# Neighbour lists ahead of the layers: the product of adjacency and column numbers on GpSimd, one block ahead of VectorE's Max8

## The chip, the cores and the metric

The kernel runs on one NeuronCore of a Trainium2 chip. The metric is the device time of one execution in microseconds (us); the time of a kernel is the median of its runs. TensorE multiplies matrices and transposes, VectorE and ScalarE do elementwise work and reductions, GpSimd does elementwise work too and issues the gathers, SyncE issues loads. Each engine works through its own queue in the order in which the program was written, and stops at an instruction whose semaphores are not there yet.

## The reference: a graph network of four layers

The inputs are `x`, 3327 nodes of 256 features, and `adj`, a 3327 x 3327 matrix of zeros and ones with a one in about 1 of 208 places. Layer 0 is a graph attention with one score per row, layers 1 to 3 are transformers whose attention is masked by `adj`:

```python
# layer 0
h = x @ Wt.T + bt
s = leaky_relu(h @ Wa.T + ba, 0.2)
w = softmax(where(adj > 0, s, NEG), axis=1)
x = layernorm(x + (w @ h) @ Wp.T + bp) * gamma + beta
# layers 1, 2, 3 (8 heads of 32)
q, k, v = split(layer_norm(x, g1, be1) @ w_qkv)
scores = where(adj != 0, einsum('nhd,mhd->hnm', q, k) * SCALE, -inf)
x = x + (softmax(scores) @ v) @ w_proj + b_proj
x = x + gelu(layer_norm(x, g2, be2) @ w1 + b1) @ w2 + b2
```

## The kernel before

A row of `adj` has about 16 ones and, in the data at hand, at most 40. The kernel therefore makes, for each row, the list of its columns, and the attention of layers 1 to 3 gathers only the keys and values on that list. The program has two stages: the one ahead of the layers, which makes the lists and computes layer 0, and the three layers. (A general path for denser matrices is not taken with this data.)

Ahead of the layers the rows are worked in 26 blocks of 128, and four blocks make a group. One block goes through these steps (class `Block`):

- `load`: SyncE loads 128 rows of `adj`, as integers (`a32`, three buffers).
- `sign`: a memset sets the one column that pads 3327 to 3328 (L711; on VectorE for the first three blocks, on GpSimd for the rest), then ScalarE writes the signs as bf16 into `abf` (L714; three buffers).
- `turn`: TensorE transposes `abf` in 26 pieces and ScalarE copies them out (L723, L724). `sums` then multiplies the transposed pieces with the rows of layer 0.
- `candidates`: VectorE multiplies `abf`, seen as 16 segments of 208 columns, with the row of column numbers 1 to 208, `seg1` (L731; the product goes to `v`, of which there are two buffers). 16 Max8 instructions then take the eight largest of each segment into `cand` (L735), that is, the numbers of the columns that hold a one.
- `list`: VectorE adds to each candidate the offset of its segment (L741, L742, both with two inputs) and draws from the 128 candidates the 40 largest, eight at a time, with Max8 and a match-and-replace between them (L746, L748).

A group goes through a dozen steps of its own (class `Group`): `soft` and `mix` are the softmax weights of layer 0 (from L889 and L938 on; L892 makes the one-hot row of the number of neighbours), `add`, `norm` and `norm1` the layer norms, `turn1`, `qkv` and `store` what layer 1 needs. A plan written out by hand (`plan`) gives each of them a place: before the Max8 of some block, or before its list.

Blocks 0 to 3 are done in a lead-in, together with the projection `h` of layer 0. A loop over blocks 4 to 25 does the rest. In turn i of the loop the program issues, in this order: load and sign of block i+2, the group steps of place 2i, the candidates of block i, transposes of block i+2 and (every other turn) the sums, the group steps of place 2i+1, the list of block i. The order on each engine is the order of the program; only buffers are given out by the framework, which puts a wait in front of the first instruction that uses a buffer again. `v` also serves, under the same tag and so out of the same two buffers, some large tiles of the lead-in (`s_h_rest`, `s_h_wa`).

In the layers GpSimd issues 1344 gathers of keys and values (L1303), VectorE forms scores and weighted values (L1325, L1326, L1366), TensorE sums the values over the neighbours and does the projections. A tile's query sits in PSUM, and so do the weights of blocks with short lists (`w`); for blocks with long lists the weights are in SBUF (`sc`).

Of the kernel before, what the change touches and what calls it, by code (L numbers as in the profile page):

```python
# [9 lines left out]
BF = mybir.dt.bfloat16  # L10
# [7 lines left out]
P = 128  # L18
# [14 lines left out]
NB = (N + P - 1) // P  # L33
# [16 lines left out]
NSEG = 16  # L50
SEG = NB * P // NSEG
# [457 lines left out]
@with_exitstack  # L509
def kernel(ctx: ExitStack, tc: tile.TileContext, ins, out: bass.AP):  # L510
    nc = tc.nc
    keep = ctx.enter_context(tc.tile_pool(name="s_keep", bufs=1))
    dram = ctx.enter_context(tc.tile_pool(name="s_dram", bufs=1, space=DRAM))
    flag = keep.tile([1, 1], I32, name="flag")
    E = mybir.EngineType
    with tc.manual_schedule(engines={E.PE, E.DVE, E.Activation, E.Pool, E.SP}):
        with ExitStack() as inner:
            sparse_path(inner, tc, ins, out, dram, flag)
    unfit = nc.values_load(flag[0:1, 0:1])
    with tc.If(unfit > 0):  # L520
        general_path(tc, ins, out)


def sparse_path(ctx, tc, ins, out, dram, flag):
    nc = tc.nc
# [40 lines left out]
    class Norm:  # L566
# [18 lines left out]
        def turn(self, j, v, work, pb):  # L585

            xn = work.tile([P, D], FP, tag="xn", name=f"xn_{self.name}_{j}")
            nc.scalar.activation(xn, v, AF.Identity, bias=self.nm[:, j:j + 1],  # L588
                                 scale=self.rs[:, j:j + 1])
            for c in range(2):  # L590
                nc.tensor.transpose(pb[c][:, j * P:(j + 1) * P], xn[:, c * P:(c + 1) * P], ident)  # L591
# [31 lines left out]
    with tc.tile_pool(name="a", bufs=1) as a, tc.tile_pool(name="aw", bufs=2) as aw, \  # L623
# [10 lines left out]
        seg1 = a.tile([P, SEG], BF, name="seg1")  # L634
# [17 lines left out]
        part = a.tile([P, 1], FP, name="part")  # L652
# [41 lines left out]
        class Block:  # L694
# [21 lines left out]
            def turn(self, aT):  # L716

                i = self.i
                for k0 in range(0, NB, 7):
# [3 lines left out]
                        nc.tensor.transpose(pt[:, m, :], self.abf[:, k * P:(k + 1) * P], ident_bf)  # L723
                    nc.scalar.copy(aT[:, k0:k0 + len(ks), :], pt[:, :len(ks), :])  # L724

            def candidates(self, part=None):

                i = self.i
                if not part:
                    v = self.v = aw.tile([P, NSEG, SEG], BF, tag="v", name=f"s_v_{i}")  # L730
                    nc.vector.tensor_mul(v, self.abf.rearrange("p (s c) -> p s c", c=SEG),  # L731
                                         seg1[:, None, :].to_broadcast([P, NSEG, SEG]))
                    self.cand = aw.tile([P, NSEG, 8], FP, tag="cand", name=f"cand_{i}")
                for s in range(NSEG) if part is None else range(part * 4, part * 4 + 4):
                    nc.vector.max(out=self.cand[:, s, :], in_=self.v[:, s, :])  # L735
# [46 lines left out]
        def x_turn(g):  # L782
            blocks = GROUPS[g]
            xT = aw.tile([P, 2, 512], FP, tag="hT", name=f"s_xT_{g}")
            for c in range(2):
                pb = bank(f"s_px_{g}_{c}")
                for j, i in enumerate(blocks):
                    nc.tensor.transpose(pb[:, j * P:(j + 1) * P],
                                        x_sb[:, i, c * P:(c + 1) * P], ident)
                nc.scalar.copy(xT[:, c, :len(blocks) * P], pb[:, :len(blocks) * P])  # L790
            turned[g] = xT

        def h_of(g):
            blocks, xT = GROUPS[g], turned.pop(g)
            ph = bank(f"s_ph_{g}").rearrange("p (b h) -> p b h", h=H0)
            for j, i in enumerate(blocks):
                for c in range(2):
                    nc.tensor.matmul(ph[:, j, :], xT[:, c, j * P:(j + 1) * P],
                                     S.wtT[:, c, :], start=(c == 0), stop=(c == 1))
            full = [j for j, i in enumerate(blocks) if ROWS[i] == P]  # L800
            for j0, j1, r in ((0, len(full), P), (len(full), len(blocks), ROWS[-1])):
                if j1 > j0:
                    i0 = blocks[j0]
                    nc.vector.tensor_add(
                        S.h[:r, i0:i0 + j1 - j0, :], ph[:r, j0:j1, :],
                        S.bt_b[:r, None, :].to_broadcast([r, j1 - j0, H0]))
# [34 lines left out]
        class Group:  # L841
# [8 lines left out]
            def sums(self, half, aT):  # L850

                c0 = half * 2 * P
                for k in range(NB):
                    r = ROWS[k]
                    nc.tensor.matmul(self.pa[:, c0:c0 + 2 * P], S.hs[:r, k, :P], aT[:r, k, :],  # L855
                                     start=(k == 0), stop=(k == NB - 1))
                    nc.tensor.matmul(self.pc[:H0 + 1, c0:c0 + 2 * P], S.hs[:r, k, P:], aT[:r, k, :],
                                     start=(k == 0), stop=(k == NB - 1))
# [170 lines left out]
        blk = [Block(i) for i in range(NB)]  # L1029
# [28 lines left out]
        for g in range(NG):  # L1058
            x_turn(g)
            if g:  # L1060
                h_of(g - 1)
            if g == 2:
                turn(3)
            if g == 4:
                blk[4].load()
                blk[4].sign()
            for _ in range(2 if g > 3 else 1):
                pieces.pop(0)()
        h_of(NG - 1)
# [34 lines left out]
        def step(g, name):  # L1104
            G = groups[g]
            G.qkv(int(name[3:])) if name[:3] == "qkv" else getattr(G, name)()

        for i in range(4, NB):
            if i + 2 < NB:
                blk[i + 2].load()  # L1110
                blk[i + 2].sign()
            for s in plan[2 * i]:
                step(*s)
            blk[i].candidates()
            if i + 2 < NB:
                turn(i + 2)
                if i % 2 or i + 2 == NB - 1:
                    sums(i + 2)
            for s in plan[2 * i + 1]:
                step(*s)  # L1120
            blk[i].list()
# [512 lines left out]
```

## Time and profile before

| what | value |
|---|---|
| time, median of 3 runs | 2568.74 us (2565.74 to 2574.27) |
| profiled execution | 3158 us, span 3156.3 us |
| busy, share of the span: PE, DVE, ACT, POOL | 57%, 61%, 25%, 43% |
| L731, product on VectorE | 26 instructions, 49.0 us, 1883 ns each |
| L735, Max8 on segments | 416 instructions, 118.0 us, 360 ns each |
| L746, Max8 in the list | 130 instructions, 38.3 us, 295 ns each |
| L714, signs on ScalarE | 26 instructions, 77.4 us, 2978 ns each |
| L711, memset of the padding on GpSimd | 23 instructions, 2.2 us, 104 ns each |

The profile is of one execution, which took longer than the timed ones; it serves for shares, durations and order. PE is TensorE's matmul, PEld its weight load, DVE VectorE, ACT ScalarE, POOL GpSimd. The stage ahead of the layers takes about the first 500 us of the span, and the loop over blocks 4 to 25 of it runs from 86 us to about 455 us. A digit in the busy rows is the busy share of one of 40 equal slices, in tenths.

### The profile page before, as it was taken

How to read it: one execution, taken by the hardware profiler on the slowest of the kernel's cores; microseconds unless marked ns; L12 is line 12 of the kernel's file. 1: busy time of each engine (PE TensorE's matmuls, PEld its weight loads, DVE VectorE, ACT ScalarE, POOL GpSimd, SP SyncE). 2: the span in 40 equal slices, each digit the busy share in tenths (PEclk: the TensorE clock that was granted, in tenths of full speed). 3: DMA queues.
4: the chain of work that ended last, by engine and by line, in shares of the span. 5: the costliest groups of instructions: out<-in, count | busy, mean ns of one | idle time of the engine just before them, and what ended most of it. 6: DMA issues, size and time to landing. Idle time of an engine off the chain costs nothing.

```text
span 3156.3 us, 24036 instructions
## 1 busy us (share of the span) xinstructions
PE 1794.0 (57%) x7561; PEld 1163.5 (37%) x7561; DVE 1935.3 (61%) x3983; ACT 774.6 (25%) x1316; POOL 1362.7 (43%) x1458
## 2 busy tenths in 40 slices
PE   4767752255666666671457667666713435665556
PEld 3645531133333333350334333433512323433334
DVE  6688995457657656533656756755446556656554
ACT  4455621012222222230112212222300111212112
POOL 4000004545555554305555555544054555565550
PEclk9868766577787886785578778878755766776768
DMA  5334306645555565415455555555064554554560
GB/s 207 131 117 148 129 31 204 174 138 169 165 172 162 156 174 152 112 51 177 141 156 156 163 160 150 175 152 140 24 189 125 156 155 135 169 163 147 161 156 13
DMA packets 144486, 453.80 MB, mean 144 GB/s; under 512 B 29521, under 2 KB 40156, under 8 KB 141021
## 3 DMA queue, kind: packets, MB, share of 16 engines
q0 software_dynamic: 113056, 370.26, 40.9%
q1 hardware_dynamic: 9834, 53.90, 4.9%
q10 hardware_dynamic: 21458, 28.02, 2.5%
q8 instruction: 61, 1.00, 0.1%
q14 instruction: 77, 0.63, 0.1%
HBM read 420.64 MB, written 31.42 MB: 143 GB/s over the span
## 4 chain that ended last, share of the span: by engine, by line
DVE 25%; issue 18%; PE 18%; another core or an unknown queue 17%; POOL 11%; ACT 5%; DMA 5%; DVEq 0%; ACTq 0%; POOLq 0%; SPq 0%
POOL kv L1303 11%; DVE kv L1325 5%; DMA kv<-kv,t 4%; DVE sc L1326 3%; DVE vw L1366 3%; PE pu L1439 3%; PE po L1372 3%; PE py L1462 2%; DVE cand L735 2%; PE pk L1492 1%; PE s_pk L1010 1%; ACT s_aT L724 1%; DVE s_v L731 1%; PE pf L591 1%
## 5 line engine op out<-in xcount | busy, mean ns | idle before, releaser
L1303 POOL DMA_INDIRECT kv<-kv,t x1344 | 1273.0, 947 | 1210.3 <-issue 534.2
L1372 PE MATMUL po<-s_ident,vw 128*128 128x128 f32 x2688 | 475.4, 334 | 580.2 <-DVE vw L1366 387.2
L1372 PEld LDWEIGHTS po<-s_ident,vw 128*128 128x128 f32 x2688 | 395.5, 174 | 724.1 <-issue 373.5
L1325 DVE TENSOR_TENSOR kv<-kv,q 128x1024 f32<-128x1024 f32 (+3 forms) x363 | 413.1, 1138 | 397.1 <-ACT q L1311 274.6
L1366 DVE TENSOR_TENSOR vw<-kv,w 128x1024 f32<-128x1024 f32 x333 | 371.4, 1128 | 87.2 <-remote 84.6
L1326 DVE TENSOR_REDUCE sc<-kv 128x32 f32<-128x1024 f32 (+3 forms) x363 | 414.1, 1141 | 12.4
L1439 PE MATMUL pu<-fT,s_w 128*128 128x512 f32 (+3 forms) x768 | 341.2, 579 | 62.3 <-issue 35.8
L1462 PE MATMUL py<-gT,s_w 128*128 128x512 f32 (+2 forms) x672 | 321.8, 597 | 58.1 <-issue 50.2
L1400 DVE TENSOR_TENSOR t<-t,po 128x256 f32<-128x256 f32 x78 | 32.6, 418 | 390.8 <-remote 254.5
L1445 ACT ACTIVATE gT<-pu,pvb 128x512 f32<-128x512 f32 (+3 forms) x192 | 115.7, 607 | 628.2 <-remote 384.1
L1439 PEld LDWEIGHTS pu<-fT,s_w 128*128 128x128 f32 x768 | 157.4, 222 | 196.1 <-issue 146.4
L1462 PEld LDWEIGHTS py<-gT,s_w 128*128 128x128 f32 x672 | 132.6, 206 | 180.7 <-issue 144.0
L1396 PEld LDWEIGHTS po<-s_w_proj,oT 128*128 128x128 f32 x312 | 71.8, 255 | 281.8 <-issue 272.3
L1394 PE MATMUL po<-bias,s_ones_bf 96*128 96x256 bf16 x78 | 25.2, 324 | 259.7 <-issue 147.4
L1390 ACT COPY oT<-po 128x256 f32<-128x256 f32 x78 | 28.9, 371 | 548.5 <-remote 320.2
L711 POOL MEMSET s_abf<- 128x1 bf16 x23 | 2.2, 104 | 361.4 <-DVE s_v L731 253.7
L1492 PE MATMUL pk<-s_w_qkv,nT 128*128 128x512 f32 x208 | 128.4, 748 | 22.0 <-ACT nT L596 9.9
L735 DVE MAX8 cand<-s_v 128x8 f32<-128x208 bf16 x416 | 118.0, 360 | 0.9
L1396 PE MATMUL po<-s_w_proj,oT 128*128 128x256 f32 x312 | 113.1, 500 | 0.0
L723 PE MATMUL s_ptb<-s_ident_bf,s_abf 128*128 128x128 bf16 x676 | 67.1, 265 | 68.3 <-ACT s_abf L714 45.2
L591 PE MATMUL pf<-s_ident,xn_f 128*128 128x128 f32 x156 | 46.1, 444 | 86.8 <-ACT xn_f L588 66.7
L855 PE MATMUL s_pa<-s_aT,s_hs 128*128 128x256 bf16 x338 | 82.3, 290 | 13.2 <-DVE s_hs L817 13.2
(288 smaller groups left out, 2252.1 us busy)
## 6 DMA issues: line engine op xcount, KB each, us to landing
s_a<-in_adj_dram SPq DMA_DIRECT2D x25, 1663.5 KB
kv<-kv,t POOLq DMA_INDIRECT x1344
kv<-kvr ACTq DMA_DIRECT2D x52, 256.0 KB
kv<-s_kvr ACTq DMA_DIRECT2D x26, 256.0 KB
s_w<-in_L_gnn_w_dram SPq DMA_DIRECT2D x6, 1024.0 KB
t<-ql ACTq DMA_DIRECT2D x6, 592.0 KB
t<-s_x ACTq DMA_DIRECT2D x6, 512.0 KB
s_w_qkv<-in_L_gnn_w_qkv_dram SPq DMA_DIRECT2D x3, 768.0 KB
```

Source lines behind the costliest of these rows:

```text
L735: nc.vector.max(out=self.cand[:, s, :], in_=self.v[:, s, :])
L855: nc.tensor.matmul(self.pa[:, c0:c0 + 2 * P], S.hs[:r, k, :P], aT[:r, k, :], start=(k == 0), stop=(k == NB - 1))
L1303: nc.gpsimd.indirect_dma_start(out=t[:, s, :], out_offset=None, in_=kv[L], in_offset=bass.IndirectOffsetOnAxis(ap=t2[:, b, k:k + 1].bitcas ...
L1325: nc.vector.tensor_mul(k, k, self.q[b][:, None, :].to_broadcast([P, n, D]))
L1326: nc.vector.tensor_reduce(self.sc[b][:, s0:s0 + n, :], k.rearrange("p s (h d) -> p s h d", d=HD), AX.X, ALU.add)
L1366: nc.vector.tensor_mul(vw[:, :n * D].rearrange("p (s h d) -> p s h d", h=HEADS, d=HD), v, self.wp[b][:, s0:s0 + n, :, None].to_broadcast([ ...
L1372: nc.tensor.matmul(self.po[b][:, k * P:(k + 1) * P], vw[:, at:at + P], ident, is_transpose=True, start=(s0 + s == 0 and k == 0), stop=(s0 ...
L1396: nc.tensor.matmul(ps, c["oT"][:, k * P:(k + 1) * P], w["w_proj"][:, k, :], start=False, stop=(k == 1))
L1439: nc.tensor.matmul(c["pu", f][:, :n], w["w1"][:, e, f * P:(f + 1) * P], c["hT"][:, e, :n], start=(e == 0), stop=(e == 1))
L1445: nc.scalar.activation(g[:, :n], c.pop(("pu", f))[:, :n], AF.Gelu_apprx_tanh, bias=w["b1"][:, f:f + 1])
L1462: nc.tensor.matmul(c["py"][e][:, :n], w["w2"][:, f, e * P:(e + 1) * P], g[:, :n], start=(f == 0), stop=last)
L1492: nc.tensor.matmul(ps[:, :c1 - c0], c["hT"][:, e, j * P:(j + 1) * P], nxt["w_qkv"][:, e, c0:c1], start=(e == 0), stop=(e == 1))
```

## The change

The product of L731 becomes a function of its own, `weigh`, which takes the engine. For blocks 0 to 3 VectorE makes the product as before. For blocks 4 to 25 GpSimd makes it, and the call stands one turn of the loop earlier: in turn i, ahead of the group steps and of the Max8 of block i, GpSimd is given the product of block i+1. Block 4's is issued in the lead-in, as soon as its sign has been. The purpose is to take the product off VectorE, which has most of the work here, and to have it ready when the Max8 need it. Nothing else is changed: the Max8, the lists and all buffers with their number stay. After the change GpSimd's queue in the loop is, turn by turn, the memset of L711 for block i+2 and the product of block i+1; VectorE's queue is as before without the 22 products. A product waits for the sign of its block (ScalarE) and for a free `v`, that is, for the last Max8 of the block two before it; the first Max8 of a block waits for GpSimd.

```diff
+            def weigh(self, engine):
+
+                v = self.v = aw.tile([P, NSEG, SEG], BF, tag="v", name=f"s_v_{self.i}")
+                engine.tensor_mul(v, self.abf.rearrange("p (s c) -> p s c", c=SEG),
+                                  seg1[:, None, :].to_broadcast([P, NSEG, SEG]))
+
             def candidates(self, part=None):
 
                 i = self.i
+                if i < 4 and not part:
+                    self.weigh(nc.vector)
                 if not part:
-                    v = self.v = aw.tile([P, NSEG, SEG], BF, tag="v", name=f"s_v_{i}")
-                    nc.vector.tensor_mul(v, self.abf.rearrange("p (s c) -> p s c", c=SEG),
-                                         seg1[:, None, :].to_broadcast([P, NSEG, SEG]))
                     self.cand = aw.tile([P, NSEG, 8], FP, tag="cand", name=f"cand_{i}")
...
             if g == 4:
                 blk[4].load()
                 blk[4].sign()
+                blk[4].weigh(nc.gpsimd)
...
             if i + 2 < NB:
                 blk[i + 2].load()
                 blk[i + 2].sign()
+            if i + 1 < NB:
+                blk[i + 1].weigh(nc.gpsimd)
             for s in plan[2 * i]:
                 step(*s)
             blk[i].candidates()
```

## The prediction

> **What bounds the kernel now.** I read the busy rows over the span first, to find where the change lies, then the windows of that stage, VectorE's waits in it, and last the instructions in order of time.
>
> The page's second part has one digit for each 78.9 us:
>
> ```profile
> PE   4767752255666666671457667666713435665556
> DVE  6688995457657656533656756755446556656554
> POOL 4000004545555554305555555544054555565550
> ```
>
> The change lies in slices 1 to 6, ahead of the layers: VectorE (DVE) is the fullest engine there and GpSimd (POOL) is empty until the gathers start. The windows answer cuts the stage finer; its columns are the window, its length, busy us of PE, PEld, DVE, ACT and POOL with the number of instructions, the TensorE clock, the DMA share and GB/s:
>
> ```profile
> 86.00:118.00 32.00, 26.97 (x240) 24.82 (x239) 16.67 (x52) 13.36 (x13) 0.20 (x2) 0.88 0.37 123
> 118.00:200.00 82.00, 50.62 (x368) 39.71 (x367) 67.57 (x257) 42.37 (x51) 0.41 (x4) 0.69 0.34 122
> 200.00:300.00 100.00, 75.44 (x493) 56.61 (x491) 81.89 (x288) 60.35 (x78) 0.61 (x6) 0.80 0.43 150
> 300.00:400.00 100.00, 71.17 (x518) 55.59 (x515) 93.49 (x341) 60.24 (x73) 0.61 (x6) 0.80 0.37 124
> 400.00:455.00 55.00, 28.98 (x168) 19.89 (x169) 51.82 (x203) 17.64 (x31) 2.97 (x2) 0.69 0.11 40
> ```
>
> VectorE is busy 295 of the 337 us between 118 and 455, and what it really waits for there is little (engine and line, waited for, us, times, longest):
>
> ```profile
> DVE s_z L938 <- ACT s_m L919: 7.6, 2, 4.4
> DVE s_x L972 <- PE s_pp L963: 6.8, 3, 5.0
> DVE deg L889 <- ACT s_acc L876: 6.1, 1, 6.1
> DVE place L927 <- PE places L903: 5.6, 2, 2.9
> DVE s_x L986 <- ACT s_x L980: 1.5, 1, 1.5
> ```
>
> 27.6 us in all; the remaining 14 us or so are gaps of 0.03 to 0.2 us between dependent small instructions. So an instruction more or less on VectorE moves the end of the stage, and the layers start after it. One block in order of time (start, us, engine, line, operation):
>
> ```profile
> 308.67 1.88 DVE L731 TENSOR_TENSOR s_v<-s_abf,seg 128x3328 bf16<-128x3328 bf16 x1
> 310.59 4.53 DVE L735 MAX8 cand<-s_v 128x8 f32<-128x208 bf16 x16
> 315.15 0.29 DVE L741 SCALAR_TENSOR_TENSOR ctmp<-cand,off 128x128 f32<-128x128 f32 x1
> 315.48 0.29 DVE L742 TENSOR_TENSOR ctmp<-cand,ctmp 128x128 f32<-128x128 f32 x1
> 315.81 0.29 DVE L746 MAX8 lists<-ctmp 128x8 f32<-128x128 f32 x1
> ```
>
> The product takes 1.88 us, the 16 Max8 4.53 us, the list after them 3.8 us, then the group's steps. What matters below: L741 and L742, right after the last Max8, each read two tiles from SBUF.
>
> [...] beside GpSimd's gathers a product with both inputs in SBUF is no slower than one with its weights in PSUM (`w`):
>
> ```profile
> L1366 DVE TENSOR_TENSOR vw<-kv,w 128x1024 f32<-128x1024 f32 x279 | 336.4, 1215 | 87.2 <-remote 84.6 <-PE pk L1492 0.9
> L1366 DVE TENSOR_TENSOR vw<-kv,sc 128x1024 f32<-128x1024 f32 x30 | 35.0, 1221 | 10.9 <-PE po L1372 10.9
> ```
>
> [...] ahead of the layers GpSimd does only memsets. [...]
>
> **The change part by part.** Removed from VectorE: 22 products, blocks 4 to 25. The Max8 follow at 1.92 us after the product's start, so 22 x 1.92 = 42 us. Block 4's share buys nothing: after it VectorE waits for ScalarE's sign of block 5 until 108.0. Blocks 6 to 25 give 20 x 1.92 = 38 us.
>
> Added on GpSimd: 22 products of 128x3328 bf16, two inputs in SBUF. The trace has no such row. [...] for the upper end I take a quarter more, 9.0 us, should bf16 or the repeated row `seg1` cost something. GpSimd's one-input select of 128x128 in the trace, 0.29 us for 128, would be 7.5 us for 3328, on the same scale. I take 7.3.
>
> Queue and waits: GpSimd's queue is now memset of block i+2, product of block i+1. The product waits for the sign of i+1 and for one of two `v` buffers, that is for the last Max8 of block i-1. It is needed at the first Max8 of block i+1, after list i-1, Max8 i and list i: 3.8 + 4.5 + 3.8 = 12 us at least, so 7.3 us are in time and 9.0 too. Behind the product stands the next memset, and behind that ScalarE's sign two blocks ahead; the memset waited for VectorE's product before, so this is about even: nothing. One product is on the path whatever happens: block 5's sign ends at 107.96, so its Max8 start at 108.0 + 7.3 + 0.15 = 115.4 and not at 109.99, 5.4 us later. Without contention: 5.4 - 38 = -33 us.
>
> [...] the last Max8 of block i-1 releases the GpSimd product. GpSimd's memset started 0.15 us after the product it waited for (310.55 to 310.70). L741 starts at 0.03 us and lasts 0.29, [...] and L742, due 0.04 us later, stands until the product is through. That is 7.3 - 0.1 = 7.2 us, once in nearly every block of 7 to 25. Where the group's softmax steps come between (five blocks), its first two-input instruction, L892, is due 0.4 us on: the same. For block 6, and in part 7, the product is set by a late sign and falls on Max8 and waits. I laid GpSimd products of 7.3 us over VectorE's 380 us of instructions by these rules: 135 us of standing, or 18.7 x 7.2. Sum: -33 + 135 = +102. While VectorE stands, TensorE and ScalarE go on, and of its 27.6 us of waits those that do not hang on its own last instruction, half, go: -14. Result +88 us, 2568.7 + 88 = 2657. [...] with 9.0 it is +140 - 14 = +126 (2695).
>
> The layers are unchanged, in order and in instructions. The profiled execution is longer (3156 us) than the timed ones, and the profile doesn't show where; VectorE's rows in this stage are plain arithmetic, and I take their us as those of the timed runs.
>
> **The rivals.**
> Faster, no contention: two-input instructions of VectorE and GpSimd run side by side. For it speaks that the product has 12 us of room and GpSimd is idle. The gain is at most 33 us. In parts of the stage the chain goes through TensorE and ScalarE (the chain of waits between 90 and 460 gives the product 6.4%, 23.7 us, not 42), so at least 24 - 5 = 19. Middle: -27, 2542. [...]
> Late lock: [...] so L742 slips by. Then 3.1 us of one-input list and, where no steps follow, 4.5 us of Max8 hide the product, and only blocks with steps stand. The same laying-over gives +24, less 14: +10, 2579. The memset's 0.15 us speaks against it; a product may need longer to start than a memset.
> GpSimd as the bound: it would take a product above 12 us. Nothing prices it so high; it would be 2700 and more.
>
> **How the numbers follow.** Contention from L742 on 0.52, late lock 0.12, no contention 0.33, GpSimd the bound 0.03. The time is the first's, 2657. The range must reach into the no-contention case, whose chance is above 0.2: 2534 to 2705 leaves out the best part of that case (0.1) and the top of the first (0.06). Slower by over 0.3% (7.7 us): the first and the last case, 0.55, and half of the late lock, 0.61; the late lock's other half is split between within 0.3% and faster, 0.03 each; of the no-contention case 0.03 ends within 0.3% and 0.30 faster. So within 0.3%: 0.06; faster: 0.33.
>
> **What would show it.** Right: 22 GpSimd TENSOR_TENSOR near 7 us; 22 fewer L731 on VectorE; gaps of some 7 us ahead of L742 (or L742 itself long), ending as a GpSimd product ends, with Max8 at its old 0.36 us; the stage's end, 455 before, at 540 or so. Wrong: L742 at 0.29 us beside a running GpSimd product (no contention), or standing only in group steps (late lock). A product far from 7.3 us scales the result by 19 us for each us.

## The result, and the profile after: 56 us longer, nearly all of it ahead of the layers

| what | before | after |
|---|---|---|
| time, median | 2569.88 us (2565.74 to 2574.27, 4 runs) | 2626.36 us (2624.96 to 2630.80, 4 runs) |
| ratio | | 1.0222, 95% interval 1.0201 to 1.0244 |
| last Max8 on segments ends, in the profile | 453.0 us | 505.7 us |
| first gather of the layers | 504.5 us | 556.9 us |

The change makes the kernel slower by 56.5 us; the interval of the ratio puts it between 52 and 63 us. The stage ahead of the layers is 52.7 us longer at its last Max8 and 52.4 us longer at the first gather. The few us that remain can't be placed: the profiled execution of the kernel before is longer in its layers than any timed one, so the layers of the two traces can't be compared. From the first gather to the end, the profiled execution after takes 2070 us (2627.1 less 556.9), and a timed one of before about 2065 (2569.9 less the 504.5 of the stage), which is an estimate.

The busy rows of the page after, a digit for each 65.6 us:

```profile
PE   5558665523676887787156887778633655775676
DVE  6699999957879888873588888888537877777863
POOL 5233333137777777750677676767127767776770
```

GpSimd is no longer empty ahead of the layers (digits 3 in slices 3 to 7), and VectorE is full there. The windows answer of the kernel after, with the columns as for the kernel before:

```profile
118.00:200.00 82.00, 44.71 (x344) 36.30 (x342) 71.85 (x241) 38.23 (x45) 30.82 (x10) 0.67 0.28 102
200.00:300.00 100.00, 70.78 (x451) 54.46 (x449) 95.78 (x261) 55.02 (x73) 32.65 (x10) 0.76 0.42 147
300.00:400.00 100.00, 63.66 (x394) 47.82 (x395) 96.20 (x242) 45.83 (x56) 39.13 (x12) 0.74 0.32 113
400.00:500.00 100.00, 62.00 (x362) 45.11 (x362) 95.02 (x302) 40.03 (x56) 28.89 (x7) 0.69 0.18 56
```

From 200 us on VectorE is busy 95 or 96 of every 100 us, though it has 22 instructions fewer, and its waits for others have nearly gone (engine and line, waited for, us, times, longest):

```profile
DVE s_z L943 <- ACT s_m L924: 3.3, 1, 3.3
DVE deg L894 <- ACT s_acc L881: 1.6, 1, 1.6
DVE place L932 <- PE places L908: 1.1, 1, 1.1
DVE s_x L977 <- issue: 0.2, 1, 0.2
```

These are 6.2 us where there were 27.6. So the time is in VectorE's own instructions, and the instructions in order of time show in which. First one block on VectorE, then GpSimd in the same stretch:

```profile
331.95 4.52 DVE L740 MAX8 cand<-s_v 128x8 f32<-128x208 bf16 x16
336.50 0.29 DVE L746 SCALAR_TENSOR_TENSOR ctmp<-cand,off 128x128 f32<-128x128 f32 x1
336.83 6.46 DVE L747 TENSOR_TENSOR ctmp<-cand,ctmp 128x128 f32<-128x128 f32 x1
343.32 0.29 DVE L751 MAX8 lists<-ctmp 128x8 f32<-128x128 f32 x1
```

```profile
336.64 6.50 POOL L729 TENSOR_TENSOR s_v<-s_abf,seg 128x3328 bf16<-128x3328 bf16 x1 [13.30 <-DVE cand L740]
```

L747 is the line that was L742: the second instruction of the list, with two tiles from SBUF. It took 0.29 us and takes 6.46 us here. The last Max8 ends at 336.47, GpSimd's product starts 0.17 us later, in the middle of L746, and ends at 343.14; 0.15 us after that L747 is done. L746 ahead of it and the Max8 behind it have their old 0.29 us. Where the group's softmax steps come between, the first instruction with two inputs after the product's start is L897 (L892 before), and it is the one that is held. L896 started 0.06 us before that product, at 393.39, and L912 comes after its end, so these two say nothing of instructions with one input:

```profile
393.33 0.17 DVE L896 TENSOR_SCALAR s_top<-deg 128x4 f32<-128x4 f32 x1
393.53 6.51 DVE L897 TENSOR_TENSOR OH<-num,s_top 128x164 bf16<-128x164 f32 x1
399.96 0.16 DVE L912 TENSOR_SCALAR s_non<-deg 128x4 f32<-128x4 f32 x1
```

The groups of the loop give the whole count, first those of the kernel before (118 to 453 us), then those of the kernel after (118 to 506 us):

```profile
L742 DVE TENSOR_TENSOR ctmp<-cand,ctmp 128x128 f32<-128x128 f32 x20 | 5.8, 292 | 0.7
L892 DVE TENSOR_TENSOR OH<-num,s_top 128x164 bf16<-128x164 f32 (+1 forms) x7 | 2.2, 318 | 0.2
```

```profile
L729 POOL TENSOR_TENSOR s_v<-s_abf,seg 128x3328 bf16<-128x3328 bf16 x20 | 129.7, 6483 | 227.3 <-DVE cand L740 160.4 <-DVE deg L894 31.0 <-ACT s_aT L724 13.3
L747 DVE TENSOR_TENSOR ctmp<-cand,ctmp 128x128 f32<-128x128 f32 x20 | 79.8, 3988 | 0.7
L897 DVE TENSOR_TENSOR OH<-num,s_top 128x164 bf16<-128x164 f32 (+1 forms) x7 | 33.1, 4730 | 0.2
```

L747 takes 79.8 us where L742 took 5.8 in the same 20 blocks, and L897 33.1 where L892 took 2.2: 74.0 and 30.9, together 104.9 us of standing. They are 12 instructions of L747 and 5 of L897, about 6.17 us each: GpSimd's 6.48 us less the 0.3 us that the instruction takes anyway.

Two shorter cases add 3.0 us. One is an instruction with two inputs, L943, held for 1.9 us. The other is a copy of 128x4 with one input, which takes 1.25 us where its usual time is 0.15; it ends as the product beside it does (116.23 to 122.72):

```profile
121.53 1.25 DVE L894 COPY deg<-s_acc 128x4 f32<-128x4 f32 x1 [1.56 <-ACT s_acc L881]
```

### The profile page after: what moved, and what is told of

The parts are those of the page before. It is cut to its first block, busy times and chain, and to the rows that moved or that the text cites. A ratio compares the mean times of both kernels' runs of the same rounds, so it can differ in the third digit from the quotient of the medians.

```text
span 2625.2 us, 24056 instructions
## 1 busy us (share of the span) xinstructions
PE 1694.4 (65%) x7561; PEld 1135.1 (43%) x7561; DVE 2009.3 (77%) x3961; ACT 781.2 (30%) x1316; POOL 1503.6 (57%) x1480
## 4 chain that ended last, share of the span: by engine, by line
DVE 14%; DMA 13%; PE 10%; POOL 9%; issue 8%; ACT 2%; DVEq 0%; POOLq 0%; ACTq 0%
DMA kv<-kv,t 12%; POOL kv L1311 9%; DVE kv L1333 4%; DVE vw L1374 3%; DVE sc L1334 3%; PE pu L1447 3%; PE py L1470 2%; PE po L1380 2%; PE pk L1500 1%; POOL out_dram L1513 0%; PE pq L1500 0%; DMA out_dram<-t,perm 0%; DVE t L1488 0%; PE py L1463 0%; PE po L1404 0%
## 5 line engine op out<-in xcount | busy, mean ns | idle before, releaser
L1380 PE MATMUL po<-s_ident,vw 128*128 128x128 f32 x2688 | 453.1, 327 | 497.4 <-DVE vw L1374 495.9
L1380 PEld LDWEIGHTS po<-s_ident,vw 128*128 128x128 f32 x2688 | 379.7, 169 | 626.3 <-DVE vw L1374 487.8
L1447 PE MATMUL pu<-fT,s_w 128*128 128x512 f32 (+3 forms) x768 | 321.5, 554 | 5.9 <-ACT gT L1453 3.3
L729 POOL TENSOR_TENSOR s_v<-s_abf,seg 128x3328 bf16<-128x3328 bf16 x22 | 142.6, 6482 | 287.8 <-DVE cand L740 160.4
L1470 PE MATMUL py<-gT,s_w 128*128 128x512 f32 (+2 forms) x672 | 286.6, 555 | 0.0
L1500 PE MATMUL pk<-s_w_qkv,nT 128*128 128x512 f32 x208 | 118.7, 700 | 7.2 <-ACT nT L596 7.2
L588 ACT ACTIVATE xn_f<-t,nm_f,rqy_f 128x256 f32<-128x256 f32 x78 | 43.0, 593 | 202.4 <-DVE nm_f L582 196.1
L723 PEld LDWEIGHTS <-s_abf 128*128 128x128 bf16 x676 | 60.2, 128 | 88.5 <-ACT s_abf L714 69.2
L1348 ACT ACTIVATE sc<-sc,mx 128x120 f32<-128x120 f32 (+6 forms) x78 | 32.0, 410 | 221.8 <-DVE mx L1345 219.0
L1404 PE MATMUL po<-s_w_proj,oT 128*128 128x256 f32 x312 | 96.9, 440 | 0.0
```

The lines of the kernel that those rows point to most:

```text
L729: engine.tensor_mul(v, self.abf.rearrange("p (s c) -> p s c", c=SEG), seg1[:, None, :].to_broadcast([P, NSEG, SEG]))
L1380: nc.tensor.matmul(self.po[b][:, k * P:(k + 1) * P], vw[:, at:at + P], ident, is_transpose=True, start=(s0 + s == 0 and k == 0), stop=(s0 ...
L1447: nc.tensor.matmul(c["pu", f][:, :n], w["w1"][:, e, f * P:(f + 1) * P], c["hT"][:, e, :n], start=(e == 0), stop=(e == 1))
L1470: nc.tensor.matmul(c["py"][e][:, :n], w["w2"][:, f, e * P:(e + 1) * P], g[:, :n], start=(f == 0), stop=last)
L1500: nc.tensor.matmul(ps[:, :c1 - c0], c["hT"][:, e, j * P:(j + 1) * P], nxt["w_qkv"][:, e, c0:c1], start=(e == 0), stop=(e == 1))
```

## The experiments: what holds VectorE, and where a GpSimd product costs nothing

The theory, from the trace after: a VectorE instruction with two inputs in SBUF stands until a GpSimd instruction that reads SBUF is through (L747, 6.46 us instead of 0.29); the changed kernel releases its GpSimd product just where two such instructions come next. The rivals: the loss is queueing (late signs, Max8 that wait for a slow engine); GpSimd slows VectorE whatever either of them does; only two-input instructions of both engines clash. All line numbers are those of each kernel, which shift by a few; names of tiles tell what is what. "Standing" is the time that instructions of the loop take above their usual duration. The edits are shown against the changed kernel, but those of the memset and the copy against the kernel with the product on both engines, and those of the last kernel and of the one without a product against the kernel before. The kernels were timed in groups with a kernel before in each (median 2569.9 us for the changed kernel, 2570.2 for the four below it, 2566.6 for the last three), so each ratio is to its own.

| kernel | time, us | ratio to before, 95% interval | last Max8 ends, us | standing, us |
|---|---|---|---|---|
| before | 2566.6 to 2570.2 | | 453.0 | 0 |
| after | 2626.4 | 1.0222 (1.0201 to 1.0244) | 505.7 | 108 |
| product on both engines | 2670.4 | 1.0395 (1.0365 to 1.0426) | 551.4 | 115 |
| GpSimd memset instead | 2579.4 | 1.0032 (1.0012 to 1.0052) | 459.6 | 13 |
| GpSimd copy instead | 2604.8 | 1.0140 (1.0110 to 1.0169) | 488.2 | 45 |
| no product | (other gathers) | | 432.3 | 0 |
| candidates in PSUM | 2614.5 | 1.0182 (1.0153 to 1.0210) | 498.2 | 42 |
| product released after L742 | 2574.7 | 1.0025 (1.0017 to 1.0033) | 457.1 | 27 |
| product in two pieces | 2554.5 | 0.9949 (0.9928 to 0.9969) | 435.0 | 2 |

**The product on both engines.** GpSimd's work is put in without anything being taken out, so queueing and standing come apart.

```diff
-                if i < 4 and not part:
-                    self.weigh(nc.vector)
+                if not part:
+                    self.weigh(nc.vector) if i < 4 else self.product(nc.vector)
```

`product` is the multiplication of `weigh` alone, into the buffer that GpSimd has filled already.

> GpSimd makes the products of blocks 4 to 25 where the changed kernel has them, and VectorE makes them again, as before the change, into the same buffer; so nothing is taken off VectorE. Theory (VectorE's two-input instructions stand while a GpSimd product reads SBUF): the 17 standings of the changed kernel come back whole, L742 and L892 at about 6.5 us, 105 us in all, less about 20 us of waits that go: last Max8 at about 545 us instead of 453, time about 2660. Rival (the loss comes from late signs or from Max8 waiting for GpSimd): VectorE never waits for GpSimd's result here except at block 5, so 2570 to 2580.

The groups of its loop:

```profile
L732 POOL TENSOR_TENSOR s_v<-s_abf,seg 128x3328 bf16<-128x3328 bf16 x20 | 130.6, 6531 | 87.8 <-DVE cand L743 46.6 <-DVE deg L897 27.9 <-ACT s_aT L724 9.0
L750 DVE TENSOR_TENSOR ctmp<-cand,ctmp 128x128 f32<-128x128 f32 x20 | 85.9, 4295 | 0.7
L732 DVE TENSOR_TENSOR s_v<-s_abf,seg 128x3328 bf16<-128x3328 bf16 x21 | 39.5, 1881 | 17.2 <-POOL s_abf L711 17.2
L900 DVE TENSOR_TENSOR OH<-num,s_top 128x164 bf16<-128x164 f32 (+1 forms) x7 | 33.1, 4731 | 0.2
```

L750 is L742. 13 of its 20 instructions and 5 of L900 stand, about 6.2 us each, as in the changed kernel, and VectorE waits 17.2 us for GpSimd's queue (L711), once, at block 5, where it waited 11.3 us for the sign before. The time is 100 us above the kernel before, 10 more than expected, as 115 us stood and not 105. Queueing as the cause is out; it would have been 10 us. The run shows the other order of the two engines as well: a GpSimd product that starts at 118.32, while VectorE's own product is running (117.54 to 119.43), takes 7.45 us instead of 6.48. There it is GpSimd that stands.

**A GpSimd memset in its place.** Writes only.

```diff
-                self.product(engine)
+                if engine is nc.gpsimd:
+                    nc.gpsimd.memset(v, 0.0)
+                else:
+                    self.product(engine)
```

> As the run before, with a GpSimd memset of the whole product buffer in the place of the GpSimd product: it only writes SBUF. Theory [...]: no standing, L742 at 0.29 us, last Max8 at 453 to 456, time 2565 to 2580. Rival (whatever GpSimd does in SBUF holds VectorE): L742 stands for the memset's length, some 3 us, 17 times, 50 us less waits: about 2605.

The memset on GpSimd (duration in ns, least, median and most), then groups of VectorE in the loop:

```profile
L730 POOL MEMSET s_v<- x22: 2872/2872/2896, 40.0 to 423.1; 128x3328 bf16 x22
```

```profile
L902 DVE TENSOR_SCALAR s_top<-deg 128x4 f32<-128x4 f32 (+1 forms) x7 | 14.6, 2085 | 0.2
L753 DVE TENSOR_TENSOR ctmp<-cand,ctmp 128x128 f32<-128x128 f32 x21 | 6.1, 291 | 0.7
L903 DVE TENSOR_TENSOR OH<-num,s_top 128x164 bf16<-128x164 f32 (+1 forms) x7 | 2.2, 318 | 0.2
```

L753 (L742), with two inputs, keeps 291 ns, and 13 of its instructions ran wholly inside a memset of 2.87 us: this GpSimd memset, which only writes, does not hold it. L903 (L892) has its 318 ns too, but none of its seven ran beside a memset, so it shows nothing here. Something stands, which I had not expected: L902, a tensor_scalar of 128x4 with one input, takes 2.85 us in five of seven cases, 13 us in all. Why it stands where the two-input L753 doesn't no view shows. The last Max8 ends 6.6 us later than before and not 0 to 3 us, as expected; the 13 us of standing, less waits that go, fit that, but no run takes them away.

**A GpSimd copy in its place.** One input read, in the same place.

```diff
-                self.product(engine)
+                if engine is nc.gpsimd:
+                    nc.gpsimd.tensor_copy(v, self.abf.rearrange("p (s c) -> p s c", c=SEG))
+                else:
+                    self.product(engine)
```

> As the run before, with a GpSimd copy of the signs into the product buffer: one input read from SBUF, instead of two. Theory: a read is a read, so L742 and L892 stand for the copy's length, about 3 to 4 us, 17 times, 50 to 60 us less some 15 us of waits: 2605 to 2615. Rival (only GpSimd instructions with two inputs clash): no standing, 2570 to 2580.

```profile
L730 POOL COPY s_v<-s_abf 128x3328 bf16<-128x3328 bf16 x19 | 56.5, 2974 | 92.5 <-DVE cand L746 51.0 <-DVE deg L900 27.8 <-issue 8.5
L753 DVE TENSOR_TENSOR ctmp<-cand,ctmp 128x128 f32<-128x128 f32 x20 | 37.5, 1873 | 0.7
L903 DVE TENSOR_TENSOR OH<-num,s_top 128x164 bf16<-128x164 f32 (+1 forms) x7 | 15.5, 2215 | 0.2
```

L753 and L903 stand again, 12 and 5 times, as long as the copy is, 2.97 us. So one input read by GpSimd is enough here; a second one on its side is not needed. The 45 us of standing are a little less than the 50 to 60 expected, and the time, 2604.8 us, is at the lower end of 2605 to 2615.

**No product at all.** What the change could bring if GpSimd cost nothing.

```diff
-                    v = self.v = aw.tile([P, NSEG, SEG], BF, tag="v", name=f"s_v_{i}")
-                    nc.vector.tensor_mul(v, self.abf.rearrange("p (s c) -> p s c", c=SEG),
-                                         seg1[:, None, :].to_broadcast([P, NSEG, SEG]))
+                    if i < 4:
...
+                    else:
+                        self.v = self.abf.rearrange("p (s c) -> p s c", c=SEG)
```

> The kernel before with the product left out for blocks 4 to 25: Max8 works on the signs, so the lists hold wrong columns and the layers gather other rows; only the stage ahead of the layers is to be read. It is what the change could have brought at best, with no GpSimd work at all. Removed are 20 x 1.92 = 38 us that count. If VectorE's chain alone sets the stage, the last Max8 ends at 453 - 38 = 415 us; if TensorE and ScalarE take over where the chain goes through them, at 429 or so (24 us less).

The Max8 of blocks 4 to 25 (duration, then first and last start):

```profile
L739 DVE MAX8 cand<-s_abf x352: 354/358/378, 85.9 to 431.9; 128x8 f32<-128x208 bf16 x176
```

The last Max8 ends at 432.3 us instead of 453.0, near the 429 expected if TensorE and ScalarE take over in places. 20.7 us of the 38 that VectorE is spared arrive. For the rest VectorE waits for these two: 47.8 us from 118 us to the last Max8, where it waited 27.6 us in the kernel before. (The Max8 also hold the buffer of the signs longer than the product did; what that costs is not shown.)

**The candidates in PSUM.** The moment of the product stays as in the changed kernel; only the number of SBUF inputs of the two list instructions changes, and where the Max8 write.

```diff
-                    self.cand = aw.tile([P, NSEG, 8], FP, tag="cand", name=f"cand_{i}")
+                    c0 = 256 + i % 2 * 128
+                    self.cand = places[:, c0:c0 + 128].rearrange("p (s k) -> p s k", k=8)
```

> The changed kernel with the candidates in PSUM instead of SBUF, so L741 and L742 (L746 and L747 there) have one SBUF input each; everything else, the moment of the GpSimd product too, is as in the changed kernel. Theory: L747 no longer stands (0.3 us instead of 6.46, 12 times, 74 us less); L897 in the softmax steps still does (5 times, 31 us), and norm1, which comes 3.8 us after the product's start, stands for some 2.6 us in five blocks: about 44 us of standing instead of 105. With the waits that come back the time is 2580 to 2595, against 2626. Rival (GpSimd's product slows VectorE whatever its operands): L747 or the instruction after it stays at 6.5 us, time 2626.

One list with a GpSimd product beside it, in order of time:

```profile
357.14 0.29 DVE L747 SCALAR_TENSOR_TENSOR ctmp<-places,off 128x128 f32<-128x128 f32 x1
357.28 6.47 POOL L729 TENSOR_TENSOR s_v<-s_abf,seg 128x3328 bf16<-128x3328 bf16 x1 [11.10 <-ACT s_aT L724]
357.46 0.29 DVE L748 TENSOR_TENSOR ctmp<-places,ctmp 128x128 f32<-128x128 f32 x1
357.79 0.29 DVE L752 MAX8 lists<-ctmp 128x8 f32<-128x128 f32 x1
```

L748 is L742, now with its candidates from PSUM: 0.29 us in the middle of a GpSimd product. It is the same addition, at the same place behind the same Max8, beside the same product, and it no longer stands: 12 of its instructions ran inside a product, all in 0.29 us. That settles what holds it: the second input from SBUF. What still stands is mainly what should, the softmax step's L898 and norm1's L992, 31 and 11 us (below, with the Max8):

```profile
L741 DVE MAX8 places<-s_v 128x8 f32<-128x208 bf16 x334 | 128.7, 385 | 10.9
L898 DVE TENSOR_TENSOR OH<-num,s_top 128x164 bf16<-128x164 f32 (+1 forms) x7 | 33.1, 4734 | 0.2
L992 DVE TENSOR_TENSOR s_x<-s_x,s_brow 128x1024 f32<-128x1024 f32 x5 | 17.1, 3410 | 0.0
```

The time was missed, though: 2614.5 where 2580 to 2595 was expected. With its output in PSUM the Max8 is dear, 6.69 us for 16 instead of 4.53, in each of the 22 blocks, with a GpSimd product beside it or without,

```profile
332.78 6.69 DVE L741 MAX8 places<-s_v 128x8 f32<-128x208 bf16 x16
```

which is 43 us over 20 blocks, and VectorE waits another 15.5 us for TensorE's additions into the same tile (`places`). Of the 65 us of standing that were saved, these two take back some 58.

**The product released later.** The product of block i+2 is asked for behind L742 of list i, so that one-input instructions come next.

```diff
+                if late:
+                    nc.vector.memset(v[:, 0, 0:1], 0.0)
...
                 nc.vector.tensor_add(tmp, cand, tmp)
+                if 4 <= i < NB - 2:
+                    blk[i + 2].weigh(nc.gpsimd, late=True)
...
-            if i + 1 < NB:
-                blk[i + 1].weigh(nc.gpsimd)
+            if i == 4:
+                blk[5].weigh(nc.gpsimd)
```

> The changed kernel with the GpSimd product of block i+2 released after L742 of list i (a one-column memset by VectorE right behind L742 releases it), and not at the last Max8 before it. Theory: the 3.1 us of one-input list that follow, and the Max8 where no steps come between, run beside it; mix and norm1 come too early and stand about 3.2 us each, twice in a group of four blocks, 32 us in all instead of 105. The best that taking the product off can bring is 21 us (stage without product), so 2570 to 2585. Rival (standing does not depend on which instructions come next): 105 us as before, 2626.

```profile
L995 DVE TENSOR_TENSOR s_x<-s_x,s_brow 128x1024 f32<-128x1024 f32 x6 | 18.2, 3031 | 2.7 <-ACT s_x L989 2.7
L947 DVE TENSOR_TENSOR s_z<-deg,s_m 128x4 f32<-128x4 f32 (+1 forms) x7 | 13.7, 1953 | 13.4 <-ACT s_m L928 13.4
L749 DVE TENSOR_TENSOR ctmp<-cand,ctmp 128x128 f32<-128x128 f32 x20 | 5.8, 292 | 0.7
```

L749 (L742) is at 292 ns, since the product starts behind it. mix (L947) and norm1 (L995), which the expectation named, stand for the remainder of the product, 12.6 and 10.9 us, and the copy of `deg` twice, 3.1 us in all: once beside a product and once, 2.13 us, beside the memset of 32 rows (L713 in the kernel before), which only writes. With the same engines doing the same work, a loss of 8 us against its own before is left of the 56: the loss was in which instruction came next.

**The product in two pieces.** Each piece is laid into a stretch in which VectorE reads one tile at a time.

```diff
+                if 5 <= i < NB - 1:
+                    blk[i + 1].new_v()
+                    blk[i + 1].late(0, CUT)
...
                 nc.vector.tensor_add(tmp, cand, tmp)
+                if 5 <= i < NB - 1:
+                    blk[i + 1].late(CUT, NSEG)
```

The part that leaves blocks 4 and 5 on VectorE is not shown. `new_v` takes the buffer; `late(s0, s1)` is a one-column memset on VectorE and then the product of segments s0 to s1 on GpSimd; CUT is 10.

> The GpSimd product in two pieces, each released by a one-column memset of VectorE and laid into a stretch in which VectorE has one input: segments 0 to 9 of block i+1 (4.05 us) under the 16 Max8 of block i (4.53 us), segments 10 to 15 (2.43 us) behind L742 of list i under the rest of that list (3.1 us); blocks 4 and 5 stay on VectorE. Theory: nothing stands, so the stage comes within 3 to 5 us of the one without a product (last Max8 at 432): 435 to 438, time 2550 to 2556, faster than both kernels. Rival (GpSimd beside VectorE costs as such, or the pieces overrun): standings of L741, L742 or slower Max8, time 2570 or more.

The start of one block in order of time, then the groups of the loop:

```profile
313.33 0.06 DVE L740 MEMSET s_v<- 128x1 bf16 x1
313.55 4.12 POOL L733 TENSOR_TENSOR s_v<-s_abf,seg 128x2080 bf16<-128x2080 bf16 x1 [13.03 <-DVE s_v L740]
313.59 4.23 DVE L755 MAX8 cand<-s_v 128x8 f32<-128x208 bf16 x15
```

```profile
L733 POOL TENSOR_TENSOR s_v<-s_abf,seg 128x2080 bf16<-128x2080 bf16 (+1 forms) x40 | 133.4, 3334 | 190.5 <-DVE s_v L740 160.1 <-ACT s_abf L715 16.8 <-ACT s_sc L887 12.0
L755 DVE MAX8 cand<-s_v 128x8 f32<-128x208 bf16 x336 | 94.8, 360 | 0.0
L762 DVE TENSOR_TENSOR ctmp<-cand,ctmp 128x128 f32<-128x128 f32 x20 | 5.8, 292 | 0.7
L761 DVE SCALAR_TENSOR_TENSOR ctmp<-cand,off 128x128 f32<-128x128 f32 x20 | 5.8, 289 | 0.5
```

The first piece, 4.12 us, lies under 16 Max8 that keep their 360 ns; L761 and L762 (L741 and L742) run between the two pieces and keep 289 and 292 ns. One instruction still stands for long, the copy of `deg`, 2.34 us beside a first piece. The last Max8 ends at 435.0 us, 2.7 us from the kernel without a product. At 2554.5 us it is faster than its own before by 0.5% (0.3 to 0.7%), that is by 12 us, where the changed kernel is 56 us slower than its own. Its last Max8 is 18 us earlier than before, so some 6 us do not arrive in the time; where they go is open.

## Why the prediction was right, and what was mis-sized

Forecast was slower by 88 us, measured 56.5. The range of 2534 to 2705 us reached from a gain of 35 us to a loss of 136, so that the time lies in it says little (and by its own greatest gain of 33 us it left out nothing of the case without contention, though it claims to leave out a tenth). What bears the forecast out is that the named instructions stood, at the named moment. Point by point:

- **That VectorE bounds the stage** held in the kernel after: from 200 us on it was busy 95 to 96 of 100 us. But "an instruction more or less on VectorE moves the end of the stage" is right for more only: in the kernel without a product 38 us less on VectorE moved the end by 20.7.
- **What is taken off** (20 times 1.92, 38 us) is counted in full in the sum below, which closes to 1 us; that fits a kernel in which VectorE hardly waits. **Block 5's product on the path** came as forecast, but that its Max8 start at 115.45, forecast 115.4, is luck: the sign ended 0.85 us later than in the trace before (108.81), and the product was 0.82 us shorter than the 7.3 taken.

```profile
108.94 6.48 POOL L729 TENSOR_TENSOR s_v<-s_abf,seg 128x3328 bf16<-128x3328 bf16 x1 [42.46 <-ACT s_abf L714]
115.45 4.52 DVE L740 MAX8 cand<-s_v 128x8 f32<-128x208 bf16 x16 [19.97 <-POOL s_abf L711]
```

- **The contention at L742 and L892** is shown, by the trace after (an instruction that ends with GpSimd's product, 17 times) and by the runs: it comes with a GpSimd read (product on both engines, copy), not with a GpSimd write (memset), and goes with the second SBUF input (candidates in PSUM). The moment was right too: the product starts 0.17 us behind the last Max8, forecast 0.15. No run had shown the standing of L742 and L892 when it was forecast, nor that the rest of a list is free of it; the run in two pieces shows the latter (295, 276 and 92 ns beside the second piece; 295, 275 and 92 in the kernel before). The prediction did not reckon with the instructions with one input that stand as well, L894 in the kernel after (1.25 us instead of 0.15) and L902 beside the memset (2.85 us instead of 0.17).
- **The trace before did show the contention**, in the other order, and the prediction overlooked it. GpSimd does not do only memsets ahead of the layers: it also issues 26 gathers (L658) in the first 41 us, and each reads its row numbers from a tile in SBUF (`rows_i`). Of the first 25, the three that start during a product of VectorE take 2.57, 2.38 and 2.09 us and end 0.8 us after that product; the others take 0.94 to 1.14. (The 26th, of 127 rows, takes 2.56 us with no product beside it and is left aside.) In the trace after, where two of the 25 start during a product at other moments, they take 1.53 and 2.39 us. The first of the three, with the gather ahead of it and VectorE's product:

```profile
12.96 0.95 POOL L658 DMA_INDIRECT s_x<-in_x_dram,rows_i  x1 [0.30 <-issue]
14.21 2.57 POOL L658 DMA_INDIRECT s_x<-in_x_dram,rows_i  x1 [0.30 <-issue]
14.06 1.89 DVE L731 TENSOR_TENSOR s_v<-s_abf,seg 128x3328 bf16<-128x3328 bf16 x1 [9.85 <-ACT s_abf L714]
```

- **The reading of L1366** (1221 ns against 1215) shows little of how the two engines run side by side: none of those 30 products overlaps a gather, and at most three overlap one of GpSimd's indirect stores (L1505, 0.97 and 1.18 us). What a GpSimd instruction that only writes does is read from the memset run.
- **The term that was mis-sized is the 135 us of standing.** It measured 104.9. The product takes 6.48 us and not 7.3, which was an assumption next to the 7.5 us scaled from the select, and by the prediction's own 19 us for each us that is 16 us. Each standing is 0.3 us shorter than the product, and not 0.1, which is 3 to 4 us more. The rest, some 10 us, is the count: 17 instructions stood, where 18.7 had been laid out. The products of blocks 6 and 7 fell on Max8, waits and the two shorter cases; that of block 8 started at 143.21, 0.19 us after L747 had, and held nothing: the late rival, once. The 9.0 us assumed for the upper end held.
- **The waits that go** were put at 14 us, by the guess that half of them hang on VectorE itself; 21 us went, so this term was too small by 7.
- The sum with measured terms is 5.5 - 38.4 + 104.9 - 21.4 = 50.6, and 3.0 us on two instructions of the first group's steps (L894, L943): 53.6, against 52.7 at the last Max8. So the end of the stage, 505.7 us and not some 540, misses by the same terms.
- **The rival without contention** was put at 19 to 33 us of gain. The stage without a product ends 20.7 us earlier, and it doesn't pay the 5 us for block 5's product, so some 15 us would have been left, by estimate, less than the lower end of 19. The chain through TensorE and ScalarE, with its 24 us, came nearer than VectorE's own sum of 38.
- **The late rival**, in which L742 has begun before GpSimd's product does, was forecast at 2579. The kernel that releases the product behind L742, which comes near to it, is 8 us above its own before, forecast 10.
- As a sign, "gaps ahead of L742 or L742 itself long": it is the second. The standing is inside the instruction's duration, so it shows as a busy VectorE and not as a wait.

## What to carry to other kernels

Before work goes from VectorE to GpSimd, look at what VectorE executes beside it and not only at whether GpSimd is idle: in these runs an addition with two SBUF inputs stood until the GpSimd product or copy beside it was through (6.46 us beside the product, where it takes 0.29 alone), and so did a small copy with one input (1.25 us instead of 0.15); a small tensor_scalar and that copy stood even beside a memset (2.85 and 2.13 us). The busy share hides this (VectorE 95 to 96 of 100 us), and an average over a line does too (3988 ns for L747); here a duration that ends with GpSimd's instruction gave it away. If the work must go there, release it by a small instruction of VectorE's own at the start of a stretch of Max8 and list instructions with one input, and cut it to fit the stretch: here that made the difference between 56 us lost and 12 us gained.

## What the runs showed of the hardware that was not expected

- A GpSimd memset that only writes held a VectorE tensor_scalar of 128x4 for 2.85 us, while two-input additions beside such a memset ran in 0.29 us. A copy of 128x4 (`deg`) was held for 2.13 us in the late run by a memset, and for 1.25 us in the changed kernel by a product.
- Where one of the two stood, it was the one that came later, on either engine: three gathers of GpSimd stood behind VectorE's product in the kernel before (2.09 to 2.57 us instead of 0.95), and a GpSimd product behind VectorE's in the run with both (7.45 us instead of 6.48).
- GpSimd's product of bf16 costs 1.95 ns for a column of 128 elements (6.48 us for 3328), its copy 0.89 ns (2.97 us), and its memset 2.87 us for 3328 columns, the same on 128 partitions (memset run) as on 32 (L713 in the kernel before). A piece of 2080 columns takes 4.12 us and one of 1248 takes 2.54, so a cut costs about 0.2 us.
- Max8 of 208 bf16 columns comes every 0.28 us with its output in SBUF and every 0.42 us with its output in PSUM (4.53 and 6.69 us for 16).
